# Three DMA queues dealt out anew, and longer runs of x, in a two-layer pre-activation network

## The chip, the cores and the metric

The kernel runs on one NeuronCore of a Trainium2 chip, in a single launch. The metric is the device time of a run in microseconds (us), as the median of several runs. Below, PE is TensorE, DVE is VectorE, ACT is ScalarE, POOL is GpSimd, and SP is SyncE; a "queue" is the list of transfers that one of SP, ACT and POOL issues.

## The reference

The input x is one image of 384 channels and 192 x 192 pixels in float32. Two layers are added to it in turn, each fed by a group norm of 32 groups without weights.

```python
# layer 0: channel attention at half resolution
x = x + L0(gn(x))
#   qkv = maxpool2x2(w_qkv @ . + b_qkv); 3x3 depthwise convolution; q, k normalized over pixels
#   attn = q k^T (8 heads of 48 channels); the sum of 4 softmaxes over the top 24, 32, 36, 38 entries
#   gelu(attn @ v), repeated 2x2, then w_proj @ . + b_proj
# layer 1: binary convolution with shifts
x = x + L1(gn(x))
#   xb = sign(.), channel c is shifted along the row by (c + 3) % 7 - 3 pixels, zeros at the borders
#   out = sign(weight) @ shifted + bias
```

## The kernel before

The image is cut into 24 units of 8 rows. A unit's tile `xt` has 128 partitions x 3 channel tiles x 1536 pixels of float32, 2304 KB in all, and a partition holds 18 KB of it. In device memory a unit lies as 3 x 128 x 1536, so that one partition's share is three runs of 6 KB. `unit(u)` (L111 to L114) takes a buffer and has SP load the unit.

The work has five stages. Stage 1 loads all 24 units and takes the statistics of the first group norm on DVE (`bn_stats`, L183); ACT loads the weights and small parameters meanwhile. Stage 2 goes over the units again, computes q and k (matmuls at L237, max pool at L244, the depthwise convolution at L258 and L260) and gathers the products of q and k. Stage 3, the ranking and the four softmaxes, is woven into stage 4, which goes over the units for v and applies the attention (L415). The result stays on the chip in six tiles `chunk`, one for every four units. The pool `big` has eight buffers, which x tiles and chunks share.

Stage 5, the last, works on one unit after the other, from the last chunk of the image back to the first. Two units are still in their buffers from stage 4, and a pool `more` gives two further buffers. For each unit there are two steps.

- `signed(i)` multiplies the chunk with the projection (PE L514, tile `yps`), adds the result to x in place (DVE L523, six operations), and writes the signs as 8-bit floats into `signs` (ACT L526, three operations, one for each channel tile m). The rows of `signs` have gaps, so that a shift along the row is a copy at another offset. Fourteen SBUF-to-SBUF transfers then bring the signs, shifted, into `moved` (L538). The list `SHIFTS` holds seven moves of 16 partitions with all channel tiles in a run of 4700 bytes, six moves of 7 partitions with one channel tile, and one of 2 partitions. The seven large ones are issued by ACT and the seven small ones by POOL.
- `finished(i)` multiplies `moved` with the signs of the weights (PE L554, 36 matmuls into `l1ps`), adds the result to x (DVE L562), and has POOL store the unit (L568; L566 for the last unit, in three parts). Then `loads()` asks SP for the next unit into the buffer that the store will set free.

The order of stage 5 is written out by hand (`manual_schedule`): `signed(i + 1)` stands before `finished(i)` on every engine, and `signs` and `moved` have two copies each. After every fourth `signed` a chunk is no longer needed, and its buffer also goes to a load.

In the program as built, every transfer of SP or ACT takes one of eight completion semaphores in turn, and every transfer of POOL one of eight others. Before it is issued, a transfer waits until the one that had its semaphore last has landed, which is the transfer eight places earlier in that turn. SP's loads and ACT's moves share the first eight, and POOL's moves and the stores share the second eight. So on the list of waits the seventh large move of unit 6 (counted from 0 in stage 5) waits for a load, and every store waits for the store before it.

Of the kernel before, what the change touches and what calls it, by code (L numbers as in the profile page):

```python
# [10 lines left out]
F32 = mybir.dt.float32  # L11
# [6 lines left out]
P = 128  # L18
C = 384
CT = C // P  # L20
# [4 lines left out]
HD = C // HEADS  # L25
# [3 lines left out]
NU = H // UR  # L29
UPX = UR * W  # L30
# [4 lines left out]
SP = 16  # L35
# [7 lines left out]
CPX = CR * WP  # L43
NCH = NU // UC
NST = NU * (UPX // 512) * 6
NBIG = 8
MORE = 2
KEEP = 6
RESIDENT = NBIG - NCH
TOPK = 1  # L50
# [41 lines left out]
@with_exitstack  # L92
def conv_preact_kernel(ctx: ExitStack, tc: tile.TileContext, a: dict, out: bass.AP):
    nc = tc.nc
    xv = a["x"].rearrange("u t p n -> u p t n")
    ov = out.rearrange("u t p n -> u p t n")


    const = ctx.enter_context(tc.tile_pool(name="const", bufs=1))

    big = ctx.enter_context(tc.tile_pool(name="big", bufs=NBIG))

# [5 lines left out]
    nmean1 = const.tile([P, CT], F32, name="nmean1")  # L108
    wb = const.tile([P, CT, C], F8, name="wb")

    def unit(u, pool=big):  # L111
        xt = pool.tile([P, CT, UPX], F32, name="xt", tag="big")
        nc.sync.dma_start(xt, xv[u])
        return xt  # L114

# [44 lines left out]
    kept = {}  # L160
    with tc.tile_pool(name="p1", bufs=1, side="right") as p1, tc.tile_pool(name="p1ps", bufs=2, space=PSUM) as psp:
        stats = p1.tile([P, CT, NST], F32, name="stats0")
        grp = p1.tile([P, CT, C], F32, name="grp_s0")
        for u in reversed(range(NU)):
            xt = unit(u)
# [14 lines left out]
            for t in range(CT):  # L180
                for j in range(UPX // 512):
                    i = (u * (UPX // 512) + j) * 6
# [42 lines left out]
    def rows(u):  # L225

        return (1 if u else 2), (PR if u < NU - 1 else PR + 1)
# [37 lines left out]
    with tc.tile_pool(name="p2w", bufs=1, side="right") as wp, tc.tile_pool(  # L265
        name="p2t", bufs=2, side="right"
    ) as tp, tc.tile_pool(name="p2qkv", bufs=3, space=PSUM) as pqkv, tc.tile_pool(
        name="p2tr", bufs=2, space=PSUM
    ) as ptr, tc.tile_pool(name="p2g", bufs=1, space=PSUM) as pg:
        pool = padded(wp, 2 * CT)  # L270
        dwo = [wp.tile([P, (PR + 1) * WP], F32, name=f"dw{m}") for m in range(2 * CT)]
        gram = [pg.tile([P, 512], F32, name=f"gram{t}") for t in range(CT)]
        for u in range(NU):
            xt = kept.pop(u) if u in kept else unit(u)
            lo, hi = rows(u)
            n = hi - lo + 1
# [29 lines left out]
    def softmaxes(p3, psp):  # L306
# [33 lines left out]
            yield  # L340

        rank = p3.tile([P, CT, HD], F32, name="rank")
        both = big.tile([P, 2, HD, HD], F32, name="both", tag="big")
        gt, eq = both[:, 0], both[:, 1]
        for t in range(CT):
            row = at[:, t, :]
            other = row.unsqueeze(1).to_broadcast([P, HD, HD])
# [47 lines left out]
    chunk = []  # L395
    with ExitStack() as vs:
        wp = right("p4w", stack=vs)
        p3 = right("p3", stack=vs)
        pqkv = vs.enter_context(tc.tile_pool(name="p4qkv", bufs=3, space=PSUM))
        po = vs.enter_context(tc.tile_pool(name="p4o", bufs=3, space=PSUM))  # L400
        psp = vs.enter_context(tc.tile_pool(name="p3ps", bufs=2, space=PSUM))
        pool = padded(wp, CT)
        wl = wp.tile([P, CT, C], F32, name="wl")
        nc.scalar.dma_start(wl, a["weightT"].rearrange("(t p) o -> p t o", p=P))
        nc.scalar.activation(wb, wl, AF.Sign, saturate=False)
        todo, steps = [], None

        def attention(c):
            for b in range(CPX // ABLK):
                cols = slice(b * ABLK, (b + 1) * ABLK)  # L410
                pss = []
                for t in range(CT):
                    ps = po.tile([P, ABLK], F32, name="ops")
                    for k in MEET[t]:
                        nc.tensor.matmul(  # L415
                            ps,
                            aT[:, k, t * P : (t + 1) * P],
                            chunk[c][:, k, cols],
                            start=(k == MEET[t][0]),
                            stop=(k == MEET[t][-1]),  # L420
                        )
                    pss.append(ps)
                for t in range(CT):
                    i = c * (CPX // ABLK) + b
                    nc.scalar.activation(chunk[c][:, t, cols], pss[t], AF.Gelu, accum_out=osum[:, t, i : i + 1])

        for u in range(NU):
            xt = unit(u)
            if u >= NU - RESIDENT:
                kept[u] = xt  # L430
            if u % UC == 0:
                chunk.append(big.tile([P, CT, CPX], F32, name="chunk", tag="big"))
            lo, hi = rows(u)
            first = PR * u - 2 + lo
            last = first + hi - lo
            for m in range(CT):
                parts = []
                for c in range(first // CR, last // CR + 1):
                    r0, r1 = max(first, c * CR), min(last, c * CR + CR - 1)
                    parts.append(  # L440
                        (chunk[c][:, m, (r0 - c * CR) * WP : (r1 + 1 - c * CR) * WP], r0 - first, r1 + 1 - r0)
                    )
                qkv_unit(pqkv, xt, u, 2 * CT + m, pool[m], parts)
                if u >= TOPK and steps is None:
                    steps = softmaxes(p3, psp)
                if steps:
                    steps = steps if next(steps, 1) is None else ()
            if last // CR > first // CR or u == NU - 1:
                todo.append(first // CR)
            if steps == ():  # L450
                while todo:
                    attention(todo.pop(0))
# [27 lines left out]
    with ExitStack() as last:  # L480
# [3 lines left out]

        more, sp = opened("p5x", MORE), opened("p5s", 1)
        pyp, psp = opened("p5py", 2, space=PSUM), opened("p5ps", 3, space=PSUM)
# [8 lines left out]
        home = {u: big for u in kept}  # L495

        def loads():
            while free and todo:
                u = todo.pop(0)
                home[u] = free.pop(0)  # L500
                kept[u] = unit(u, home[u])

        def signed(i):

            u = order[i]
            xt = kept[u]
            o = chunk[u // UC][:, :, u % UC * PPX : (u % UC + 1) * PPX]
            x5 = xt.rearrange("p t (i a j b) -> p t a i j b", a=2, b=2, j=WP)
            sg, mo = signs[i % 2], moved[i % 2]
            rows3 = sg[:, LEAD : LEAD + CT * SLEN].rearrange("p (t r w) -> p t r w", r=UR, w=PITCH)  # L510
            for m in range(CT):
                ps = pyp.tile([P, PPX], F32, name="yps")
                for t in range(CT):
                    nc.tensor.matmul(  # L514
                        ps,
                        wpr[:, t, m * P : (m + 1) * P],
                        o[:, t, :],
                        start=(t == 0),
                        stop=(t == CT - 1),
                    )  # L520
                yb = ps.rearrange("p (i j) -> p i j", j=WP).unsqueeze(3).to_broadcast([P, PR, WP, 2])
                for r in range(2):
                    nc.vector.scalar_tensor_tensor(  # L523
                        x5[:, m, r], yb, bpr[:, m : m + 1], x5[:, m, r], ALU.add, ALU.add
                    )
                nc.scalar.activation(  # L526
                    rows3[:, m, :, :W],
                    xt[:, m, :].rearrange("p (r w) -> p r w", w=W),
                    AF.Sign,
                    bias=nmean1[:, m : m + 1],  # L530
                    saturate=False,
                )
            to = mo.rearrange("p t r w -> p (t r w)")
            for p0, n, t0, nt, dx in SHIFTS:
                run = nt * SLEN - (PITCH - W)
                at = t0 * SLEN
                queue = nc.scalar if n == SP else nc.gpsimd
                queue.dma_start(  # L538
                    to[p0 : p0 + n, at : at + run], sg[p0 : p0 + n, LEAD + dx + at : LEAD + dx + at + run]
                )  # L540
            if i % UC == UC - 1:
                free.append(big)
                loads()

        def finished(i):

            u = order[i]
            xt, mo = kept.pop(u), moved[i % 2]
            for m in range(CT):
                for r0 in range(0, UR, 4):  # L550
                    ps = psp.tile([P, 2, 512], F32, name="l1ps")
                    for j in range(2):
                        for t in range(CT):
                            nc.tensor.matmul(  # L554
                                ps[:, j, : 2 * W],
                                wb[:, t, m * P : (m + 1) * P],
                                mo[:, t, r0 + 2 * j : r0 + 2 * j + 2, :W],
                                start=(t == 0),
                                stop=(t == CT - 1),
                            )  # L560
                    blk = xt[:, m, r0 * W : (r0 + 4) * W].rearrange("p (j n) -> p j n", j=2)
                    nc.vector.scalar_tensor_tensor(  # L562
                        blk, ps[:, :, : 2 * W], bl1[:, m : m + 1], blk, ALU.add, ALU.add
                    )
                if i == NU - 1:
                    nc.gpsimd.dma_start(ov[u, :, m], xt[:, m])  # L566
            if i < NU - 1:
                nc.gpsimd.dma_start(ov[u], xt)  # L568
            free.append(home[u])
            loads()  # L570

# [78 lines left out]
```

## Time and profile before

| | us |
|---|---|
| median of 3 runs | 2528.49 (2528.05 to 2529.06) |
| profiled execution, device time | 2525.06 |
| its span, from first to last instruction | 2523.3 |
| stage 1 and the steps behind it, until the first matmul of stage 2 | 190.2 |
| stages 2 to 4 | 190.2 to 2108 |
| stage 5, from its first matmul to the end | 2113.3 to 2523.3 |

All further times are microseconds from the start of the span. The profile is one execution, recorded by the hardware. A row of a table of groups gives the line, the engine, the operation, its tiles (out<-in) and their count, then the busy time, the mean of one in ns, and the idle time of the engine just before them with what ended it. "ACTq" and "SPq" are transfers that an engine's sequencer issues. The time to landing runs from the start of a transfer's issue until its completion semaphore has its full count. Queue q1 is SP's, q10 is ACT's and q0 is POOL's.

### The profile page before, as it was taken

Reading aid. Unit: us, or ns where it says so; the run is one execution under the profiler, and the core shown is the slowest. Engines: PE = TensorE matmul, PEld = TensorE weight load, DVE = VectorE, ACT = ScalarE, POOL = GpSimd, SP = SyncE. Lnnn points to the kernel's source line nnn. Section 1 sums busy time; section 2 is a strip of 40 time slices with the busy share of each in tenths; the row PEclk is TensorE's granted clock in tenths of the full one; section 3 lists DMA queues with packets and bytes.
Section 4 is the critical chain, followed back from the end, with each engine's and each line's share of the span. In section 5 each row is a group of like instructions: output and inputs, shape, how many; then the busy total and the mean of one; then the engine's idle time right before and its main releaser. Section 6 shows DMA issues by size and latency. Waiting matters only on the chain.

```text
span 2523.3 us, 18868 instructions
## 1 busy us (share of the span) xinstructions
PE 2232.7 (88%) x6451; PEld 1079.8 (43%) x6451; DVE 1889.7 (75%) x3115; ACT 648.9 (26%) x1282; POOL 117.0 (5%) x215
## 2 busy tenths in 40 slices
PE   0039999999999999999999999999999999767687
PEld 0034444444444444444444444444444444434344
DVE  6965777777777777777777799994686775766677
ACT  0002223233233232332233211222222212222232
POOL 0000000000000000000000000000000001222232
PEclk9999999999999999999999999999999999988999
DMA  9951111211111111201001031311121212999997
GB/s 362 418 241 38 38 38 38 75 38 38 38 52 61 38 38 38 76 0 38 38 25 50 28 113 38 150 65 48 38 77 73 75 75 80 325 328 334 331 300 228
DMA packets 60432, 285.29 MB, mean 113 GB/s; under 512 B 11536, under 2 KB 14080, under 8 KB 60208
## 3 DMA queue, kind: packets, MB, share of 16 engines
q1 hardware_dynamic: 35200, 207.62, 22.2%
q0 software_dynamic: 15008, 58.44, 5.8%
q10 hardware_dynamic: 10128, 18.02, 3.0%
q8 instruction: 51, 0.84, 0.1%
q14 instruction: 45, 0.37, 0.0%
HBM read 212.99 MB, written 56.62 MB: 107 GB/s over the span
## 4 chain that ended last, share of the span: by engine, by line
PE 45%; DVE 31%; DMA 13%; ACT 6%; issue 4%; ACTq 0%; POOL 0%; POOLq 0%; SPq 0%; DVEq 0%
PE qkv L237 32%; DVE dw L260 16%; DVE pooled L244 8%; DMA xt<-in_x_dram 6%; DMA out_dram<-xt 6%; PE ops L415 4%; DVE chunk L260 3%; PE gram L292 2%; ACT dw L258 2%; ACT pooled L251 2%; PE l1ps L554 2%; PE tr L288 2%; ACT sq L281 1%; PE yps L514 1%; DVE xt L523 1%
## 5 line engine op out<-in xcount | busy, mean ns | idle before, releaser
L237 PE MATMUL qkv<-xt,wq 128*128 128x512 f32 x3888 | 1698.5, 593 | 7.7 <-DVE pooled L244 7.4
L237 PEld LDWEIGHTS qkv<-xt,wq 128*128 128x128 f32 x3888 | 727.0, 190 | 870.9 <-issue 798.4
L260 DVE SCALAR_TENSOR_TENSOR dw<-pooled,wdw,dw 128x384 f32<-128x384 f32 (+2 forms) x1152 | 709.5, 616 | 250.9 <-ACT dw L258 226.9
L244 DVE TENSOR_REDUCE pooled<-qkv 128x128 f32<-128x512 f32 x648 | 443.2, 685 | 140.1 <-PE qkv L237 133.3
L260 DVE SCALAR_TENSOR_TENSOR chunk<-pooled,wdw,chunk 128x384 f32<-128x384 f32 (+3 forms) x696 | 361.4, 545 | 46.2 <-ACT chunk L258 34.7
L262 ACT COPY pooled<-pooled 128x196 f32<-128x196 f32 x207 | 73.7, 356 | 737.9 <-DVE dw L260 520.2
L554 PE MATMUL l1ps<-moved,wb 128*128 128x384 fp8e4 x864 | 161.9, 349 | 88.5 <-DMA moved<-signs 78.4
L251 ACT ACTIVATE pooled<-pooled,bq 128x384 f32<-128x384 f32 x216 | 133.1, 616 | 385.9 <-DVE pooled L244 385.9
L562 DVE SCALAR_TENSOR_TENSOR xt<-l1ps,bl,xt 128x768 f32<-128x768 f32 x144 | 138.0, 1011 | 95.8 <-PE l1ps L554 94.8
L526 ACT ACTIVATE signs<-xt,nmean 128x1536 fp8e4<-128x1536 f32 x72 | 112.3, 1573 | 278.4 <-DVE xt L523 143.4
L523 DVE SCALAR_TENSOR_TENSOR xt<-yps,bpr,xt 128x768 f32<-128x768 f32 x144 | 139.7, 1013 | 29.4 <-PE yps L514 29.4
L554 PEld LDWEIGHTS <-wb 128*128 128x128 fp8e4 x864 | 88.6, 104 | 165.3 <-issue 115.6
L514 PE MATMUL yps<-chunk,wpr 128*128 128x384 f32 x432 | 151.6, 498 | 4.6 <-DVE xt L523 4.6
L183 DVE BATCH_NORM_STATS2 stats<-xt 128x6 f32<-128x512 f32 x216 | 130.5, 678 | 28.6 <-DMA xt<-in_x_dram 28.5
L132 PE MATMUL gm_m<-cm,grp_s 128*128 128x1 f32 x18 | 4.0, 353 | 165.3 <-DVE cm L188 165.3
L281 ACT ACTIVATE sq<-dw 128x384 f32<-128x384 f32 (+2 forms) x144 | 75.2, 522 | 157.8 <-DVE dw L260 157.8
L514 PEld LDWEIGHTS yps<-chunk,wpr 128*128 128x128 f32 x432 | 80.8, 193 | 66.3 <-PE yps L514 18.7
L415 PE MATMUL ops<-chunk,aT 128*128 128x512 f32 x252 | 109.0, 592 | 0.0
L258 ACT ACTIVATE dw<-pooled,bdw,wdw 128x384 f32<-128x384 f32 (+2 forms) x144 | 100.8, 700 | 30.0 <-PE tr L288 28.1
L538 POOL DMA_DIRECT2D moved<-signs x168 | 87.5, 526 | 169.4 <-ACT signs L526 166.4
L288 PEld LDWEIGHTS tr<-ident,dw 128*128 128x128 f32 (+2 forms) x438 | 52.3, 140 | 70.4 <-DVE dw L260 30.9
L288 PE MATMUL tr<-ident,dw 128*128 128x128 f32 (+2 forms) x438 | 74.2, 279 | 8.8 <-DVE dw L260 8.0
(92 smaller groups left out, 525.7 us busy)
## 6 DMA issues: line engine op xcount, KB each, us to landing
xt<-in_x_dram SPq DMA_DIRECT2D x88, 2304.0 KB, 11.6
out_dram<-xt POOLq DMA_DIRECT2D x23, 2304.0 KB, 14.5
moved<-signs ACTq DMA_DIRECT2D x168, 73.4 KB, 5.1
moved<-signs POOLq DMA_DIRECT2D x144, 10.7 KB, 5.7
out_dram<-xt POOLq DMA_DIRECT2D x3, 768.0 KB, 3.7
wq<-in_w_qkvT_dram ACTq DMA_DIRECT2D x1, 1728.0 KB, 19.6
grp_s<-in_grp_dram ACTq DMA_DIRECT2D x2, 576.0 KB, 7.1
tri<-in_tri_dram ACTq DMA_DIRECT2D x1, 1152.0 KB, 7.3
```

The lines of the kernel that those rows point to most:

```text
L183: nc.vector.bn_stats(stats[:, t, i : i + 6], xt[:, t, j * 512 : (j + 1) * 512])
L237: nc.tensor.matmul(ps, wq[:, t, m * P : (m + 1) * P], x4[:, t, r0 : r0 + nr, c0 : c0 + ncol], start=(t == 0), stop=(t == CT - 1),)
L244: nc.vector.tensor_reduce(pl[:, 2 + r0 // 2 : 2 + (r0 + nr) // 2, 1 + c0 // 2 : 1 + (c0 + ncol) // 2], ps.rearrange("p (i a j b) -> p i j ...
L251: nc.scalar.activation(new, new, AF.Identity, bias=bq[:, m : m + 1])
L258: nc.scalar.activation(acc2, src, AF.Identity, bias=bdw[:, m : m + 1], scale=wdw[:, m, 0:1])
L260: nc.vector.scalar_tensor_tensor(acc2, src, wdw[:, m, k : k + 1], acc2, ALU.mult, ALU.add)
L288: nc.tensor.transpose(ps[:L, t * P : (t + 1) * P], dwo[s * CT + t][:, c0 : c0 + L], ident)
L415: nc.tensor.matmul(ps, aT[:, k, t * P : (t + 1) * P], chunk[c][:, k, cols], start=(k == MEET[t][0]), stop=(k == MEET[t][-1]),)
L514: nc.tensor.matmul(ps, wpr[:, t, m * P : (m + 1) * P], o[:, t, :], start=(t == 0), stop=(t == CT - 1),)
L523: nc.vector.scalar_tensor_tensor(x5[:, m, r], yb, bpr[:, m : m + 1], x5[:, m, r], ALU.add, ALU.add)
L554: nc.tensor.matmul(ps[:, j, : 2 * W], wb[:, t, m * P : (m + 1) * P], mo[:, t, r0 + 2 * j : r0 + 2 * j + 2, :W], start=(t == 0), stop=(t == ...
L562: nc.vector.scalar_tensor_tensor(blk, ps[:, :, : 2 * W], bl1[:, m : m + 1], blk, ALU.add, ALU.add)
```

## The change

Three things change.

1. In stage 5 POOL issues all fourteen moves of a unit, ACT issues the stores, and SP issues the loads as before.
2. In device memory a unit lies as 128 x 4608, for x and for the output, so that one partition's share is one run of 18 KB. Loads in stages 1, 2 and 4 become 128 runs of 18 KB.
3. The buffers for x become 96 bytes longer. Loads of the last stage place the three channel tiles with gaps of 32 bytes between them (`PAD` = 8 floats), so these loads and the stores from such buffers stay in pieces of 6 KB. The two units that stay from stage 4 have no gaps.

In the order of the instructions SP then issues 66 loads of 128x4608 and 22 of 128x3x1536, ACT issues two stores of 128x4608, 21 of 384x1x1536 and the three parts of the last unit, and POOL issues 336 moves. The order on PE and DVE is unchanged. POOL's eight semaphores now serve moves alone: from a unit's ninth move on, a move waits for the landing of the move eight places earlier in the same unit, and its first eight wait for moves of the unit before.

```diff
+PAD = 8
...
-    xv = a["x"].rearrange("u t p n -> u p t n")
-    ov = out.rearrange("u t p n -> u p t n")
+    xv = a["x"].rearrange("u p (t n) -> u p t n", n=UPX)
+    ov = out.rearrange("u p (t n) -> u p t n", n=UPX)
...
-    def unit(u, pool=big):
-        xt = pool.tile([P, CT, UPX], F32, name="xt", tag="big")
+    def unit(u, pool=big, pad=0):
+        xt = pool.tile([P, CT * (UPX + PAD)], F32, name="xt", tag="big")
+        xt = xt[:, : CT * (UPX + pad)].rearrange("p (t n) -> p t n", t=CT)[:, :, :UPX]
         nc.sync.dma_start(xt, xv[u])
...
-                kept[u] = unit(u, home[u])
+                kept[u] = unit(u, home[u], PAD)
...
-                queue = nc.scalar if n == SP else nc.gpsimd
-                queue.dma_start(
+                nc.gpsimd.dma_start(
                     to[p0 : p0 + n, at : at + run], sg[p0 : p0 + n, LEAD + dx + at : LEAD + dx + at + run]
                 )
...
-                    nc.gpsimd.dma_start(ov[u, :, m], xt[:, m])
+                    nc.scalar.dma_start(ov[u, :, m], xt[:, m])
             if i < NU - 1:
-                nc.gpsimd.dma_start(ov[u], xt)
+                nc.scalar.dma_start(ov[u], xt)
...
-    out = nc.dram_tensor("out_0_dram", (NU, CT, P, UPX), F32, kind="ExternalOutput").ap()
+    out = nc.dram_tensor("out_0_dram", (NU, P, CT * UPX), F32, kind="ExternalOutput").ap()
```

The tiles `both` and `chunk` take the longer buffer as well and use its first part without gaps.

More of the change, by code (lines that the diff above doesn't have):

```diff
@@ L342, in softmaxes @@
         rank = p3.tile([P, CT, HD], F32, name="rank")
-        both = big.tile([P, 2, HD, HD], F32, name="both", tag="big")
-        gt, eq = both[:, 0], both[:, 1]
+        both = big.tile([P, CT * (UPX + PAD)], F32, name="both", tag="big")
+        gt, eq = (both[:, i * HD * HD : (i + 1) * HD * HD].rearrange("p (i j) -> p i j", j=HD) for i in range(2))
         for t in range(CT):
@@ L431, in conv_preact_kernel @@
             if u % UC == 0:
-                chunk.append(big.tile([P, CT, CPX], F32, name="chunk", tag="big"))
+                ct = big.tile([P, CT * (CPX + PAD)], F32, name="chunk", tag="big")
+                chunk.append(ct[:, : CT * CPX].rearrange("p (t n) -> p t n", t=CT))
             lo, hi = rows(u)
@@ L615 @@
     ins = {
-        "x": np.asarray(x).reshape(C, NU, UPX)[xch].reshape(CT, P, NU, UPX).transpose(2, 0, 1, 3),
+        "x": np.asarray(x).reshape(C, NU, UPX)[xch].reshape(CT, P, NU, UPX).transpose(2, 1, 0, 3).reshape(NU, P, CT * UPX),
         "w_qkvT": np.asarray(L0_conv_w_qkv).T[xch],
@@ L645 @@
     r = run_bass_kernel_spmd(nc, [arrays], core_ids=[0])
-    o = np.asarray(r.results[0]["out_0_dram"]).transpose(1, 2, 0, 3).reshape(C, NU * UPX)
+    o = np.asarray(r.results[0]["out_0_dram"]).reshape(NU, P, CT, UPX).transpose(2, 1, 0, 3).reshape(C, NU * UPX)
     y = np.empty_like(o)
```

## The prediction

> **What bounds the kernel now.** I read the page first, then a table by stretches, then the waits, transfers and timeline of stage 5. The page's engine shares and its 40 slices:
>
> ```profile
> span 2523.3 us, 18868 instructions
> PE 2232.7 (88%) x6451; PEld 1079.8 (43%) x6451; DVE 1889.7 (75%) x3115; ACT 648.9 (26%) x1282; POOL 117.0 (5%) x215
> PE   0039999999999999999999999999999999767687
> DMA  9951111211111111201001031311121212999997
> ```
>
> PE is full from slice 4 to slice 34, with the DMA engines nearly idle; there a faster load is worth nothing. DMA is full in slices 1 to 3 (stage 1) and in the last seven (stage 5). Only these two stages can answer to this change. By stretches (columns: us, busy of PE, PEld, DVE, ACT, POOL, granted clock, DMA share, GB/s):
>
> ```profile
> 2113.00:2141.00 28.00, 23.85 (x78) 12.86 (x78) 17.76 (x20) 9.23 (x6) 7.39 (x14) 0.84 0.49 128
> 2141.00:2422.00 281.00, 202.05 (x864) 111.25 (x863) 183.52 (x192) 74.73 (x48) 70.88 (x128) 0.88 0.94 327
> 2422.00:2520.00 98.00, 82.41 (x359) 45.30 (x357) 75.62 (x80) 28.36 (x18) 29.03 (x52) 0.94 0.79 258
> 20.00:154.00 134.00, 0.00 (x0) 0.00 (x0) 120.00 (x199) 1.28 (x1) 0.00 (x0) 1.00 0.99 401
> ```
>
> Stage 5 has a head, a middle and a tail. The first store is issued at 2141.4, and the sixteenth, which frees the last load's buffer, lands at 2421.6. That makes 17.5 us a unit in the middle. In the tail eight units take 98 us, 12.3 each. In the middle PE is idle for 79 us of 281, although DMA moves only 327 GB/s, against 417 in stage 1 from 30 to 150. The waits of the middle (us in total, times, longest):
>
> ```profile
> ACT signs L526 <- DMA xt<-in_x_dram: 78.9, 4, 25.2
> PE l1ps L554 <- DMA moved<-signs: 66.0, 8, 20.4
> ```
>
> PE waits for moves. ACT's four long waits for a load have another cause than their name says, which the timeline shows:
>
> ```profile
> 2214.42 21.20 ACTq L538 DMA_DIRECT2D moved<-signs  x7
> ...
> 2223.51 0.90 SPq L113 DMA_DIRECT2D xt<-in_x_dram  x2
> 2223.97 0.79 POOL L568 DMA_DIRECT2D out_dram<-xt  x1 [7.75 <-DMA moved<-signs]
> 2235.83 4.50 ACT L526 ACTIVATE signs<-xt,nmean 128x1536 fp8e4<-128x1536 f32 x3 [21.43 <-DMA xt<-in_x_dram]
> ```
>
> Seven moves that take 4.4 us to issue in the tail take 21.2. Six are out by 2220.6; the seventh goes at 2235.11, just after the load issued at 2223.51 lands at 2235.09. It waits for the semaphore that this load holds, not for its data. L554 of that unit starts at 2241.5. Starts of L554 lie 12.0 to 15.9 us apart from unit 0 to 17, 14.3 in the mean, except for four gaps of 22.1, 30.9, 28.0 and 32.6. These four hold 56 us more than four ordinary ones.
>
> **Part 1a: what the new queues remove.** The moves no longer share semaphores with loads, so the four stalls go. A small move no longer sits behind a store on q0: those of unit 6 landed at 2223.8 to 2224.8, behind the store that landed at 2223.4. The store of unit i no longer waits for the landing of store i-1 (unit 13's sum was ready at 2362.2, its store went at 2367.4).
>
> **Part 1b: what they add.** POOL issues all fourteen moves after the third sign, one after the other, at 526 ns each: 7.4 us a unit, under every period above, so POOL does not bound. Yet the ninth move waits for the landing of the first, and so on. Landing takes, by the transfers of the middle and of the tail:
>
> ```profile
> moved<-signs ACTq DMA_DIRECT2D x110, 73.4 KB, 6.1
> ```
>
> ```profile
> moved<-signs ACTq DMA_DIRECT2D x35, 73.4 KB, 2.5
> ```
>
> I take ACT's rows for moves with a ring to themselves; POOL's rows in the middle (6.8 and 7.4) contain the store ahead. What is late next is a loop over two units: L554 of unit i ends; 9.8 us later the third sign of unit i+2 ends (2451.5 to 2461.3 for unit 18); then come the moves; then L554 of unit i+2, 6.2 us.
>
> - Tail: the fourteenth issue starts 0.3 + 13 x 0.526 = 7.1 us after the sign and lands 2.5 later, 9.6. Loop: 9.8 + 9.6 + 6.2 = 25.6, so 12.8 us a unit instead of 12.3. PE hides most of the longer moves. Eight units: **+4.2**.
> - Head: unit 0's moves landed 6.4 us after its sign and will need 9.6: **+3.2**. Unit 1 has slack.
> - Middle: the ninth goes at 6.1, the fourteenth some 0.6 x 5 later (ACT's spacing), and it lands at 15.2, with POOL's start at 15.5. Loop: 9.8 + 15.5 + 6.2 = 31.5, so 15.75 us a unit. Sixteen units take 252 instead of 280: **-28.0**.
>
> Bounds of the middle. Below, the packets set the floor: a 6 KB packet takes 234 ns undisturbed; the same packets and moves as now, at undisturbed times, fill 224 of the 281 us, or 14.0 a unit. Above, with a landing of 8 us (ACT's upper tenth is 8.1), the loop is 35.3, or 17.7 a unit. So -56 to +3. I take 15.75 because the median landing is measured under the same three streams.
>
> A store on ACT stands ahead of unit i+2's first sign. Its issue, about 0.4 us by SP's loads, is covered by two L523 operations of 1.01 us that this sign awaits anyway, so I price it at nothing. Without the cover it costs 24 x 0.4 = 10 us, inside the range. Its semaphore was last held by a transfer some four units old. SP's queue keeps its order.
>
> The Trainium skill's page "DMA: Bandwidth & Descriptors", section "Issuing engines are not separate DMA queues", speaks against any gain: all queues run on the same DMA engines, and spreading saves only issue time. By it the sum would keep only part 2, about 2525.7. The trace agrees on the rate (418 GB/s from one queue, up to 427 from two in slices of 5 us), not on the waits.
>
> The page "SBUF — State Buffer", section "SBUF: two separate sides", says that some DVE operations lock GpSimd out while it writes descriptors. If each of the fourteen moves waited for one DVE operation of 1.01 us, the sum would be about 60 us over the present time. The trace's issues on POOL take 521 ns median and 554 at most, with DVE busy 65% of the middle, so I leave it out.
>
> **Part 2: runs of 18 KB.** In the trace's packet records, packets of 1536, 4608, 6144 and 9216 bytes take 65, 181, 234 and 347 ns, or 8 ns + 0.0368 ns a byte. One of 18432 bytes should then take 686 ns against 3 x 234 = 702. A load now lands every 5.65 us in stage 1; eight such packets and the same 0.03 give 5.52. DVE needs 130.5 / 24 = 5.44 for a unit's nine statistics and stays just under. The first two loads come early, the third is issued at 22 behind the small parameters as now, and 21 intervals follow: 21 x 0.13 = **-2.8**. Bounds: 0, if long packets save nothing, and -4.4, where DVE binds. ACT's parameters may land later beside the longer packets; they are needed at 165. Stages 2 to 4: nothing, PE covers it (slices of 9).
>
> **Part 3: gaps.** 96 bytes a buffer and no instruction. The last stage keeps packets of 6144 bytes, so moves wait for turns of 234 ns as now, except beside two stores.
>
> **Sum.** -28.0 + 4.2 + 3.2 - 2.8 = -23.4 on the span of 2523.3, so 2499.9. The execution took 2525.06, 1.8 more than its span, and the median 2528.49 is 3.4 above that. Hence **2505.1** as a median.
>
> **Rivals.**
>
> *The DMA engines are the bound.* Packets in the middle fill 94% of 281 us = 264. If loads stay as slow beside moves as now (mean 296 ns instead of 234), sixteen units can't go below 264, 16.5 each: -16 + 4.6 = -11.4, so 2517. For: the 94%. Against: part of the 296 is the start of a load alone, which a store may cover.
>
> *Slower: POOL's eight semaphores.* The ninth move waits for the first under fuller DMA engines. At a landing of 9 us the fourteenth lands at 21.3, the loop is 37.3, 18.65 a unit: +18.4 + 4.6 = +23, so 2551. It decides from a landing of about 7.9 us on, where the period is again 17.5. For: POOL's medians of 6.8 and 7.4, and 7.3 to 8.3 us beside a fresh load at 2421.7. Against: ACT's 6.1.
>
> *The change does nothing measurable.* The stalls only let loads run ahead, and what they cost now comes back as contention: 2523 to 2533. For: the DMA engines were busy during the stalls. Against: PE's idle 79 us.
>
> **How the numbers follow.** My forecast has 0.50, the DMA bound 0.22, the slower rival 0.18 and nothing 0.10. Measurement tells about 0.2% (5 us) from no change. Faster: 0.50 + 0.22 = 0.72; same 0.10; slower 0.18. The range runs from 2478, the packet floor (2528.5 - 56 + 4.6), to 2536, which takes in the first and third rivals and the milder part of the second.
>
> **What would show it.** Right: no issue of moves stretched beyond 12 us; starts of L554 near 15.5 apart in the middle and 12.8 in the tail, without gaps of 28; the ninth move starting at the first one's landing; loads of stage 1 landing every 5.5 us. Wrong: moves landing after more than 8 us, a DMA share at 1.0 with loads above 296 ns, or signs waiting behind stores on ACT.

## The result, and the profile after

The changed kernel takes 2545.36 us (median of 4 runs, 2544.25 to 2553.23) where the kernel before took 2528.27 beside it. The ratio is 1.0079, 95% interval 1.0054 to 1.0103: slower by 0.8%, and 9 us above the range's upper end. The profiled execution took 2545.93 with a span of 2544.2, so it can stand beside the median. The page's own lines (span, then 40 slices of PE, of PE's clock and of the DMA engines):

```profile
span 2544.2 us, 18861 instructions
...
PE   0039999999999999999999999999999997766786
...
PEclk9999999999999999999999999999999998888988
DMA  9951011100110101100001121211021124999965
```

In the slices of stages 2 to 4 PE is full, as before. At the end the DMA engines are less busy than before: the last two slices are 6 and 5, where 9 and 7 stood. The stretches of stage 5 and of stage 1 (columns: us, busy of PE, PEld, DVE, ACT, POOL, granted clock, DMA share, GB/s):

```profile
2141.00:2422.00 281.00, 199.64 (x824) 108.71 (x822) 178.76 (x186) 75.62 (x48) 107.07 (x217) 0.87 0.93 326
2422.00:2520.00 98.00, 85.79 (x360) 46.69 (x360) 73.87 (x77) 28.35 (x18) 40.10 (x82) 0.91 0.62 210
20.00:151.00 131.00, 0.00 (x0) 0.00 (x0) 116.34 (x193) 1.28 (x1) 0.00 (x0) 1.00 0.98 411
```

The middle moves as many bytes as before (326 GB/s), and the tail fewer (210 instead of 258). The waits of the middle (us in total, times, longest) show what changed places:

```profile
PE l1ps L557 <- DMA moved<-signs: 69.5, 8, 12.5
POOL moved L541 <- DMA moved<-signs: 65.7, 71, 4.1
```

ACT no longer waits for a load in this stretch; its 78.9 us are gone. But POOL now waits 71 times for a move to land, 65.7 us in all, and PE waits for moves as long as before. One unit of the middle in the timeline (start, us, then the instructions; in brackets the idle time before them and its end; rows between are left out):

```profile
2222.26 1.57 ACT L530 ACTIVATE signs<-xt,nmean 128x1536 fp8e4<-128x1536 f32 x1 [0.79 <-DVE xt L527]
...
2224.12 3.88 POOL L541 DMA_DIRECT2D moved<-signs  x8 [14.32 <-ACT signs L530]
...
2231.19 0.51 POOL L541 DMA_DIRECT2D moved<-signs  x1 [3.19 <-DMA moved<-signs]
...
2236.41 0.50 POOL L541 DMA_DIRECT2D moved<-signs  x1 [0.35 <-DMA moved<-signs]
...
2243.31 3.06 PE L557 MATMUL l1ps<-moved,wb 128*128 128x384 fp8e4 x9 [10.84 <-DMA moved<-signs]
```

The third sign of unit 6 ends at 2223.83. Eight moves are out by 2228.0. The ninth goes at 2231.19, when the first has landed (2230.92), and the fourteenth at 2236.41, 1.04 us a move later. It lands at 2243.27, and L557 starts. That is 19.5 us after the sign.

I cut the span at the starts of L557 of unit 0 and unit 17:

| | before | after | difference | predicted |
|---|---|---|---|---|
| to the start of stage 2 | 190.2 | 187.0 | -3.2 | -2.8 |
| from there to L557 of unit 0 | 1942.2 | 1944.5 | +2.3 | +3.2 |
| unit 0 to unit 17 (17 units) | 299.1 | 307.1 | +8.0 | -28.0 |
| unit 17 to the end | 91.8 | 105.6 | +13.8 | +4.2 |
| span | 2523.3 | 2544.2 | +20.9 | -23.4 |

The prediction cut the middle at the first store's issue and the sixteenth store's landing, which is 280.2 us in before and 281.1 in after. Either way the gain of 28 is missing, and the tail costs three times what was said.

### The profile page after: what moved, and what is told of

Same layout as the page of the kernel before. It is cut to its first block, busy times and chain, and to the rows that moved or that the text cites. A ratio compares the mean times of both kernels' runs of the same rounds, so it can differ in the third digit from the quotient of the medians.

```text
span 2544.2 us, 18861 instructions
## 1 busy us (share of the span) xinstructions
PE 2242.8 (88%) x6451; PEld 1084.1 (43%) x6451; DVE 1890.5 (74%) x3115; ACT 649.9 (26%) x1282; POOL 175.3 (7%) x357
## 4 chain that ended last, share of the span: by engine, by line
PE 46%; DVE 33%; DMA 11%; ACT 7%; POOL 2%; issue 1%; ACTq 0%; SPq 0%; DVEq 0%; POOLq 0%
PE qkv L240 31%; DVE dw L263 16%; DVE pooled L247 8%; DMA moved<-signs 5%; PE ops L418 4%; PE l1ps L557 4%; DVE chunk L263 3%; DMA xt<-in_x_dram 3%; ACT dw L261 2%; PE yps L518 2%; PE gram L295 2%; ACT pooled L254 2%; DVE xt L527 2%; PE tr L291 2%; POOL moved L541 2%; DMA wpr<-in_w_projT_dram 1%
## 5 line engine op out<-in xcount | busy, mean ns | idle before, releaser
L557 PE MATMUL l1ps<-moved,wb 128*128 128x384 fp8e4 x864 | 172.1, 364 | 105.7 <-DMA moved<-signs 103.1
L541 POOL DMA_DIRECT2D moved<-signs x336 | 165.7, 499 | 254.3 <-ACT signs L530 174.7
L557 PEld LDWEIGHTS <-wb 128*128 128x128 fp8e4 x864 | 92.0, 108 | 189.4 <-issue 95.1
L224 POOL MEMSET pooled<- 128x686 f32 x9 | 7.4, 868 | 1426.7 <-PE tr L291 1255.3
## 6 DMA issues: line engine op xcount, KB each, us to landing
out_dram<-xt ACTq DMA_DIRECT2D x23, 2304.0 KB, 10.2
```

What stands on the lines that cost most here:

```text
L541: nc.gpsimd.dma_start(to[p0 : p0 + n, at : at + run], sg[p0 : p0 + n, LEAD + dx + at : LEAD + dx + at + run])
L557: nc.tensor.matmul(ps[:, j, : 2 * W], wb[:, t, m * P : (m + 1) * P], mo[:, t, r0 + 2 * j : r0 + 2 * j + 2, :W], start=(t == 0), stop=(t == ...
```

## The experiments

All comparisons are with the kernel before on the same chip; it had medians of 2527.5 to 2529.7. "Middle" is again L557 of unit 0 to unit 17 in the profiled execution (before 299.1, after 307.1), and "tail" the mean distance of the next five starts (before 12.6, after 15.0).

### The two halves of the change

**The layout alone**, with before's queues:

```diff
+PAD = 8
 (layout of x and out, buffers and gaps as in the change)
-                queue.dma_start(to[...], sg[...])
+                queue.dma_start(to[...].bitcast(U8), sg[...].bitcast(U8))
```

> The layout alone: x and the output in runs of 18 KB and the gaps of the last stage, with moves and stores in the queues of before (ACT's moves are named as bytes). Theory A, the new queues are what costs: stage 1 gains 3 us and nothing else moves, about 2525. Theory B, the long runs or the gaps cost in the last stage: 2540 or more. Theory C, the DMA engines bound the last stage whoever issues: 2525.

Measured: 2533.94, ratio 1.0023 (1.0014 to 1.0032). Stage 1 gains 3.2, the middle takes 307.0 and the tail 12.6. The four long gaps between starts of L554 are there as before (113 us in all in both kernels); the ordinary units are 0.6 longer on average.

**The queues alone**, with before's layout and no gaps:

```diff
-                queue = nc.scalar if n == SP else nc.gpsimd
-                queue.dma_start(
+                nc.gpsimd.dma_start(
...
-                nc.gpsimd.dma_start(ov[u], xt)
+                nc.scalar.dma_start(ov[u], xt)
```

> The new queues alone: all moves on POOL, stores on ACT, with x laid out as before. Theory A: before plus the 20 us that the changed kernel lost outside stage 1, about 2548. Theory B: about 2528, as before. Theory C: 2528 to 2532.

Measured: 2540.08, ratio 1.0045 (1.0031 to 1.006). The profiled execution was the slowest of its five (2543.94), with a span 18.9 longer than before's: 4.8 until L553 of unit 0 starts, 3.9 in the middle, 10.2 in the tail. So the queues alone cost 12 us by the medians and the layout 6, together about the change's 17. Both halves were predicted to gain.

### What the queues lose: the order of the moves and their semaphores

**The small moves first**, in after:

```diff
-            for p0, n, t0, nt, dx in SHIFTS:
+            for p0, n, t0, nt, dx in sorted(SHIFTS, key=lambda s: s[3] != 1):
```

> The changed kernel with the six moves of 7 partitions ahead of the others, so that four of them go before the third sign and ten issues are left after it. Theory A, the moves are late because fourteen are issued in a row and each waits for the one eight places earlier: in the tail the last move lands 7.3 us after the sign, ahead of the next store, and the tail comes back to 12.8 us a unit (-20); in the middle the fourteenth lands some 14.5 us after the sign instead of 19, the loop falls from 35 to 32 us (-22); together about 2503. Theory C: the tail gains 20, the middle stays at 17.5, about 2525. Theory B: 2545, no change.

Measured: 2513.25, ratio 0.9943 (0.9926 to 0.996), 32 us faster than after by one line. The middle takes 285.5, 16.8 a unit. As the expectation had it, POOL issues four small moves before the third sign, since a move waits only for the signs that it reads, and ten stand after it. The tail stays at 15.3, since the last two of the ten still go behind the next store in every second unit (store at 2455.17, moves at 2455.46 and 2455.93, landed after 5.6 and 6.8 us; those ahead of it take 1.6 to 3.0).

**Eight moves only**, in after; the six small ones are left out, so 42 partitions of `moved` stay zero:

```diff
+        for t in moved:
+            nc.gpsimd.memset(t, 0.0)
...
-            for p0, n, t0, nt, dx in SHIFTS:
+            for p0, n, t0, nt, dx in [s for s in SHIFTS if s[3] != 1]:
```

> The changed kernel with the six moves of 7 partitions left out (42 partitions of moved stay zero), so eight moves a unit, none of which waits for another of its own unit; the bytes of moves fall by an eighth only. Theory A: the last move lands 6.3 us after the sign in the tail and 10.5 in the middle, the loop of two units is 26.5 there, and the floor of the packets, 14.0 us a unit, binds: about 2466. Theory C: 16.5 us a unit in the middle, the tail as in the kernel before: about 2505.

Measured: 2488.57, ratio 0.9838 (0.9823 to 0.9853), between the two expectations. Its stretches:

```profile
2141.00:2422.00 281.00, 230.71 (x967) 126.13 (x966) 206.82 (x216) 85.06 (x54) 69.56 (x144) 0.91 0.99 353
2422.00:2520.00 98.00, 53.82 (x251) 30.22 (x249) 51.98 (x55) 18.91 (x12) 15.45 (x32) 0.96 0.45 167
```

The middle takes 269.5, 15.9 a unit, and the DMA engines are busy for 99% of it, at 353 GB/s. POOL's own wait for moves is all but gone (65.7 us in after), and eight moves are issued without a break, here for unit 7, whose third sign ended at 2229.25:

```profile
POOL moved L543 <- DMA moved<-signs: 0.8, 1, 0.8
```

```profile
2229.54 3.86 POOL L543 DMA_DIRECT2D moved<-signs  x8 [17.97 <-ACT signs L532]
...
2244.63 7.59 PE L559 MATMUL l1ps<-moved,wb 128*128 128x384 fp8e4 x28 [6.75 <-DMA moved<-signs]
```

Yet these eight land from 2236.61 to 2244.49, 1.13 us apart. In the mean of units 2 to 16 the first lands 6.5 us after the sign and the eighth 13.5, 1.0 apart; in after the first lands at 5.6 and the fourteenth at 18.2, also 1.0 apart. So the moves of one queue land at this pace whether or not they wait for a semaphore. The starts in the tail go back to 12.3 but for one.

**Small moves on ACT**, the eight others on POOL (in the program as built, two of ACT's moves go ahead of the third sign and four behind it):

```diff
-                nc.gpsimd.dma_start(
-                    to[...], sg[...]
-                )
+                queue = nc.scalar if nt == 1 else nc.gpsimd
+                dst, src = to[...], sg[...]
+                if nt == 1:
+                    dst, src = dst.bitcast(mybir.dt.uint8), src.bitcast(mybir.dt.uint8)
+                queue.dma_start(dst, src)
```

> After with the six 7-partition moves issued by ScalarE (after the three signs of the unit, ahead of the store) and the eight others by GpSimd, so that no move waits for a semaphore of its own unit and the fourteen issues go on two engines. Theory A (serial issue and the ninth move's wait are what the change lost, in the middle and in the tail): the last move lands 11 us after the third sign, the loop over two units falls to 28, below the DMA engines' 15.9 per unit that the kernel without these six showed; the middle is then DMA-bound at about 16.2 per unit, the tail goes at 12.3, and the time is 2490 to 2500. Theory B (what makes the moves slow is the streams beside them, whoever issues): landing stays at 7, and with the DMA share at 0.98 the units take 16.8 as with the small moves first, 2510. Theory C (six issues on ScalarE hold the signs and the store behind them): the third sign comes 3 us later, each unit 1 to 1.5 longer, 2520.

Measured: 2517.01, ratio 0.9955 (0.9938 to 0.9972); the expectation of 2490 to 2500 missed. The tail is exactly 12.3 a unit, as expected, but the middle takes 298.5. The timeline shows why:

```profile
2226.14 14.11 ACTq L545 DMA_DIRECT2D moved<-signs  x4
...
2246.51 0.63 ACTq L573 DMA_DIRECT2D out_dram<-xt  x1
...
2247.55 3.04 ACT L530 ACTIVATE signs<-xt,nmean 128x1536 fp8e4<-128x1536 f32 x2 [20.15 <-PE l1ps L559]
```

Four issues that take 3 us elsewhere take 14.1, until 2240.3. ACT's moves share eight semaphores with loads and stores again, as in the kernel before, and the store and the next signs stand behind them on ACT. L567 of unit 6 had ended at 2231.4; its store went at 2246.5.

**Early moves**: POOL issues the two small moves of a third of the channels as soon as its sign is there, and the large ones at the end:

```diff
             for m in range(CT):
...
+                move([s for s in SHIFTS if s[3] == 1 and s[2] == m])
-            for p0, n, t0, nt, dx in SHIFTS:
+            move([s for s in SHIFTS if s[3] != 1])
```

> After with the two 7-partition moves of a third of the channels issued by GpSimd as soon as that third's sign is there (before the next sign), and the eight others after the third sign, all still on GpSimd. The ninth move of a unit is then one that waits for a move issued 4 us before the third sign, and only eight to ten issues of 0.5 us stand after the third sign. Theory A (the ninth move's wait and the fourteen issues in a row are what the change lost): the last move lands 11 to 12 us after the third sign, the loop over two units falls to 28, the middle is bound by the DMA engines at 16.0 to 16.5 per unit, the tail goes at 12.3 to 13, and the time is 2495 to 2502. Theory B (the streams beside the moves set their landing, whatever the order): no better than the small moves first, 2513.

Measured: 2514.45, ratio 0.9939 (0.9925 to 0.9954). The expectation of 2495 to 2502 missed. As built, POOL's instructions are the same, in the same order and with the same waits, as with the small moves first, which I had not seen when I wrote it down; so this is that kernel measured once more, 1.2 us apart. It still shows what is left:

```profile
2141.00:2422.00 281.00, 223.25 (x928) 121.72 (x926) 198.32 (x207) 80.34 (x51) 118.41 (x237) 0.91 0.99 347
2422.00:2509.00 87.00, 65.08 (x296) 35.86 (x294) 62.01 (x65) 23.63 (x15) 35.65 (x72) 0.94 0.64 226
```

The middle has the DMA engines busy for 99%, at 16.5 a unit, and the tail stays at 14.8. I had counted the ninth move's wait only: the thirteenth and fourteenth wait for the two small moves that are issued after the third sign, so the last issue can stand 9 us behind it (unit 6: sign 2215.3, last issue done 2224.5).

**Early moves, and two of them on ACT**, so that POOL has four before the third sign and eight after it:

```diff
+                    if nt == 1 and t0 == CT - 1:
+                        nc.scalar.dma_start(dst.bitcast(mybir.dt.uint8), src.bitcast(mybir.dt.uint8))
+                    else:
+                        nc.gpsimd.dma_start(dst, src)
```

> The early moves, but with the two 7-partition moves of the last third issued by ScalarE, so that GpSimd has four moves before the third sign and eight after it, and the eight semaphores are enough: no move waits for one that was issued after the third sign, and the last issue stands 4.2 us after the third sign instead of 5.2 to 9. Same bytes. Theory A (the early moves alone reached the DMA engines' bound of 16.5 per unit in the middle, share 0.99; what was left to them is the tail, where the last issues still met the next unit's store): the middle stays at 16.3 to 16.5 per unit, the tail goes from a mean of 14.7 to 12.3, and the time is 2500 to 2505. Theory B (the middle was still held by the thirteenth and fourteenth move's wait): the middle falls to 16.0 as well, 2492 to 2498. Theory C (the two moves on ScalarE wait for loads and stores and hold the signs): 2515 to 2525.

Measured: 2503.33, ratio 0.9911 (0.9895 to 0.9928), the best with the change's layout:

```profile
2141.00:2422.00 281.00, 225.39 (x950) 123.18 (x949) 202.56 (x211) 83.33 (x54) 107.65 (x215) 0.92 1.00 352
```

The middle takes 273.6, 16.1 a unit, with the DMA engines busy throughout: theory B's place for the gain. The tail goes at 14.2, not at 12.3, so theory A's place for it does not hold, though its time does. POOL still waits for landings, 52 times and 33.6 us from 2141 to 2440.

### What the layout and the gaps do

**No gaps** in after, so that packets of 18432 bytes run in the last stage too:

```diff
-                kept[u] = unit(u, home[u], PAD)
+                kept[u] = unit(u, home[u])
```

> After's queues, x in 18 KB runs, and no gaps in the last stage's buffers: loads and stores there travel as 18432-byte packets too. Theory A (the gaps are what the layout costs in the last stage, where the layout alone was 10 us slower than before): 2537, and the moves land no later than 6.9 us. Theory B (a move behind an 18432-byte packet waits some 700 ns at each DMA engine where it waited 300, with three streams ahead of it): the moves' landing goes from 6.9 to 8 or 9 us, the pairs of L557 from 36 to 38 or 40, and the kernel is at 2555 to 2570. Theory C (the layout's cost lies in HBM, gaps or not): 2545 as after.

Measured: 2571.88, ratio 1.0173 (1.0153 to 1.0193), 26.5 slower than after; the middle takes 327.4. Theory B. The transfers of the middle (count, KB each, median us to landing), first after, then without gaps:

```profile
moved<-signs POOLq DMA_DIRECT2D x112, 73.4 KB, 6.9
```

```profile
moved<-signs POOLq DMA_DIRECT2D x99, 73.4 KB, 9.2
```

The large moves land 2.3 us later, while loads and stores themselves land sooner (11.9 and 8.7 instead of 13.7 and 12.9).

**The early moves without gaps** and **the split without gaps** (the same line changed):

> The same early moves, x in 18 KB runs, no gaps in the last stage. With the change's own order of moves taking the gaps away cost 26 us. Theory A (it costs only by the moves' landing in the loop over two units, 8.6 instead of 6.8, and by the ninth move's wait): the loop is 9.8 + 13.5 + 7 = 30, 15 per unit, under the DMA engines' bound, so the same as with gaps or up to 5 less. Theory B (a move behind 18432-byte packets delays the units whatever the order): 10 to 20 slower than with gaps.

> The same split, x in 18 KB runs, no gaps in the last stage. If the middle is bound by the DMA engines and fewer, longer packets cost less engine time (711 ns for 18432 bytes against three of about 300): up to 0.8 per unit less than with gaps, 2480 to 2488. If the moves wait longer behind such packets and the loop over two units is again what decides: the same or up to 10 slower than with gaps.

Measured: 2554.86 (1.0097, 1.0082 to 1.0112) and 2516.24 (0.9965, 0.9946 to 0.9984). With the early moves the missing gaps cost 40 us, twice the upper end of theory B: large moves land after 9.5 us instead of 7.3. With the split, where ACT's issues were seen to hold the store and the signs, they cost nothing that shows.

**Before's layout** (6 KB runs, no gaps) under the split, under the early moves, and under the early moves with two of them on ACT:

> The same split of the moves over ScalarE and GpSimd, with before's layout of x (6 KB runs, no gaps). If the layout costs in the last stage what the layout alone showed (0.4 to 0.5 per unit over 17 units, so 8, against 3.2 saved in stage 1): 5 faster than the split with the new layout. If that cost was only that of before's queues (the semaphore turns shifted): 3 slower than it.

> The same early moves on GpSimd with before's layout of x (6 KB runs, no gaps). Theory A (layout and gaps do not matter to the moves, only to stage 1 and to the head of the last stage): 3 to 5 slower than with the new layout. Theory B (the gaps split the packets and cost DMA time, as before's queues with the new layout suggested): 3 to 5 faster.

> The early moves with two of them on ScalarE, and before's layout of x and of the output. If the layout costs nothing in a last stage that the DMA engines bound: 3 slower than with the new layout, from stage 1, so 2506. If it costs there too: 2498 or less.

Measured: 2525.72 (ratio 0.9991, 0.9981 to 1.0), 2513.83 (0.9932, 0.9916 to 0.9949) and 2502.34 (0.9893, 0.9875 to 0.991). Against the same queues with the new layout that is 8.7 slower, 0.6 faster and 1.0 faster. The first is more than the 3 expected; the two others lie between their theories. There, where the DMA engines bound the middle, the layout is worth nothing in sum: the old one makes the middle 3.0 and 2.9 shorter in the profiled executions, and the new one saves 3 in stage 1. A difference of 3 in the middle is at the edge of what one execution can tell: with the gaps alone, which change nothing in the median, it is 302.2 against 299.1.

**One part at a time** in the kernel before: x in 18 KB runs with gaps, the output in 18 KB runs with gaps, the gaps alone.

```diff
 (only x)    xv = a["x"].rearrange("u p (t n) -> u p t n", n=UPX), gaps
 (only out)  ov = out.rearrange("u p (t n) -> u p t n", n=UPX), gaps
 (only gaps) kept[u] = unit(u, home[u], PAD)
```

> Before's queues and before's layout of the output; only x lies in 18 KB runs, and the buffers have gaps. Theory A (neighbouring 6 KB pieces of one 18 KB run make the loads of the last stage slower, and with them the moves): stage 1 gains 3, the last stage loses 8 to 10, 2533 in all, as with the whole layout. Theory B (the output's runs or the gaps do it): 2525.

> Before's queues and before's layout of x; only the output lies in 18 KB runs, and the buffers have gaps, so that stores travel in 6 KB packets. Theory A (the loads do it): 2528. Theory B (the stores do it): 2536 to 2538, the last stage 8 to 10 longer and stage 1 as before.

> Before with the gaps of 32 bytes in the last stage's buffers alone, both layouts in device memory as before. If the gaps are free, 2528, and all of the cost lies in device memory; if they cost, 2533 to 2538.

Measured, in 5 rounds: 2532.44 (1.0013, 1.0003 to 1.0023), 2529.51 (1.0003, 0.9993 to 1.0013) and 2529.00 (1.0, 0.999 to 1.0011). The gaps as such are free, and so, within what can be told, are the output's runs. x costs 4 by the medians (1 to 6 by the interval) although stage 1 gains 3, so about 7 in the last stage (4 to 9), which speaks for theory A. Why a load from an 18 KB run in 6 KB pieces disturbs the moves more than one from three runs is not settled; the load packets of the middle took 298 ns with x alone and 296 before, too small a difference to carry it.

## Why the prediction was wrong, step by step

**The four stalls of part 1a** went, as said: no issue of ACT is stretched, and no gap of 28 is left. Step right.

**Part 1b, the middle, is the step that failed.** The loop over two units is the right mechanism, and its first term holds: 9.9 from the end of L557 of unit 4 to the third sign of unit 6, and as much in every unit. The move term was mis-sized. The prediction had 6.1 to the ninth issue, 5 x 0.6 to the fourteenth, 6.1 to its landing, in all 15.5 with POOL's start. Measured in that unit are 7.4, 5.2 and 6.9: 19.5. The third term, L557, took 8.5 instead of 6.2, at a granted clock of 0.70 (2243 to 2252) after PE had waited 10.8. The loop is 37.9 instead of 31.5. In the mean of the even units from 2 to 16 it is 9.9 + 18.4 + 8.1 = 36.4: the move term was 2.9 too small, the L557 term 1.9.

The worst of the three is the spacing of 0.6, taken from ACT's issues. Those did not wait for each other; POOL's from the ninth on do, and so they go at the rate at which the first moves land. The first six of unit 6 land at 2230.92, 2231.98, 2233.27, 2234.28, 2235.27 and 2236.13, 1.04 apart, though they were issued 0.48 apart and waited for nothing; their times to landing grow from 6.8 to 9.6. The row of landings gives a median and hides the spacing: a queue's rate has to be read from two successive landings.

The semaphores delay the issue, but the trace does not show that they delay the landing. When the ninth move is issued, seven are still ahead of it in the same queue, and the eight moves of the run without small ones land 1.0 apart with no such wait. What the prediction did not price is that fourteen moves land one after the other in one queue, where before each of two queues had seven. No run had more semaphores, so that they cost nothing of their own is argued, not shown.

**The slower rival had the right sign**, at 2551 against 2545.36, but that it came so close is luck. It asked for a landing of 7.9 us or more, and the mean landing is 6.8; the spacing and the slower L557 added what the landing did not. And it put +18.4 in the middle, where +8.0 came, and +4.6 elsewhere, where +12.9 came.

**The statement that POOL does not bound** left out its waits. Unit 6 occupies POOL from 2224.1 to 2236.9, 12.8 us and not 7.4, and unit 7's first move goes right behind it at 2237.4.

**The tail's term** (+4.2) failed as well. The prediction took 2.5 us for the landing of the fourteenth move, from a row of moves whose issues had all begun before the next store (for unit 19 the last at 2452.80, the store at 2453.24). In after they are not (first the third sign of unit 19, then its moves, the store of unit 18, and L557 of unit 19):

```profile
2454.59 1.57 ACT L530 ACTIVATE signs<-xt,nmean 128x1536 fp8e4<-128x1536 f32 x1 [0.79 <-DVE xt L527]
...
2457.62 5.87 POOL L541 DMA_DIRECT2D moved<-signs  x12 [0.16 <-issue]
...
2460.09 0.56 ACTq L571 DMA_DIRECT2D out_dram<-xt  x1
...
2468.95 8.35 PE L557 MATMUL l1ps<-moved,wb 128*128 128x384 fp8e4 x36 [4.14 <-DMA moved<-signs]
```

The moves issued ahead of the store at 2460.09 land after 2.3 to 2.8 us; the six behind it take 5.1 to 6.3. L557 starts 12.8 after the sign, not 9.6, and takes 8.35. With six issues on another engine the row of the tail reads

```profile
2430.00:2502.00 72.00, 66.78 (x310) 37.77 (x309) 64.29 (x68) 26.13 (x17) 23.26 (x48) 1.00 0.75 269
```

and the starts are 12.3 apart: it is the fourteen issues in a row that cost the tail, and they were seen in the sum, but not whom they meet.

**The head** (+3.2) was right in its step: unit 0's moves land 8.9 after its sign, 9.6 predicted. L557 of unit 0 starts 0.9 earlier than before, against +0.4 by the sum.

**The stores on ACT** cost nothing, as priced. They take some 0.55 us to issue (0.56 at 2460.09), and the sign that follows is held by DVE.

**Part 2** came out: -3.2 against -2.8. Packets of 18432 bytes took 690 ns (from 60 to 100, alone on the engines), predicted 686, and the rate rose from 418 to 430 GB/s.

**Part 3 and the layout in the last stage** were priced at nothing. For the gaps themselves that is right, and so is the reason given for them, turns of 6 KB: without them the change costs 26.5 more. For the loads of x it is wrong by about 7 with before's queues.

**The DMA rival** gave 16.5 a unit as the floor. The early moves reach just that at a share of 0.99; the best order with the change's layout gets to 16.1 at 1.00, and without the six small moves it is 15.9. So with the change's layout no order that was tried reached the forecast's 15.75; with before's layout the best one came to 15.9.

**The rules of the Trainium skill.** "DMA: Bandwidth & Descriptors", section "Issuing engines are not separate DMA queues", says that the issuing engine matters only for its issue time. That all transfers share the same engines agrees with the shares of 0.99 and 1.00. That only issue time is at stake does not: with the change's layout, the same fourteen moves, loads and stores took 2545, 2513, 2517 and 2503 us by who issues them and in which order. What differs is how many moves stand behind one another in a queue after the third sign, where a wait for a semaphore holds the store and the signs as well, and what the late moves meet. The lock that the page "SBUF — State Buffer", section "SBUF: two separate sides", describes for some DVE operations does not show here either: POOL's issues took 0.48 to 0.52 us in the middle of after, while DVE was busy for 64% of it.

## What to carry to other kernels

Between an event that releases a row of transfers and the event that waits for the last of them, count the transfers in each queue, and price them at the distance of two landings, not of two issues: here 1.0 us instead of 0.48 beside a load and a store. Put what can go early ahead of the event, so that fewer remain behind it. Where transfers take completion semaphores in turn, keep those with long and short landings in different turns: an issue that waits for a load holds everything behind it on its engine. And when a change makes a burst of issues longer, ask which stream starts before it ends: the price is paid by the moves that come late.

## What the runs showed of the hardware that was not expected

- Small SBUF-to-SBUF moves of one queue, issued 0.48 us apart beside a load and a store, landed 1.0 us apart, with or without a wait for a semaphore between them; in the tail the large ones landed 2.5 us (median) after their issue.
- Packets of 18432 bytes beside such moves raised the large moves' landing from 6.9 to 9.2 us, and the DMA share of the middle fell from 0.93 to 0.88.
- With 14 moves a unit the three streams reached at most 352 GB/s in the middle at a share of 1.00, where one stream of loads in 18432-byte packets reached 430 from 60 to 100.
